# A selective-scan stack with two multiplications per job on another engine, table blocks with a settled queue ahead of them, and zeros around the closing of a sum

## The chip, the cores and the metric

The kernel runs on one core of a Trainium2 chip. A core has a matmul engine (PE, with its weight loads shown as PEld), a vector engine (DVE), a scalar engine (ACT), a general engine (POOL) and a queue that issues transfers (SP). They run side by side and wait for each other by semaphores; each works through its own instructions in program order. Matmul results lie in PSUM, which POOL does not read here; everything else lies in SBUF or in device memory. The metric is the device time of one execution in microseconds (us): lower is better.

## The reference, cut to what matters

A batch of 8 images of 192 x 56 x 56 goes through four layers, each a residual of a group norm and a block. Layer 0 is an involution. Layers 1 to 3 are selective scans over the 3136 pixels of an image, and take nearly all of the time:

```python
xc = silu(conv4(xz[:d]) + conv_b)                    # four taps along the sequence
dt, B, C = split(xc @ x_proj)                        # rank, 16, 16
delta = softplus(dt @ dt_proj + dt_b)
h = exp(delta * A) * h + delta * xc * B              # step by step along the sequence, 16 states per channel
y = (h * C).sum(over states) + xc * D
out = (y * silu(z)) @ out_proj
```

In layer 1 the 192 channels are three slices of 64 that share their weights (512 inner channels each), with layer norms over the 192 before and after and a projection behind; layers 2 and 3 have 384 inner channels.

## The kernel before

An image is cut into 7 chunks of 448 pixels. A **job** is one chunk of one sequence: in layer 1 there are three jobs per chunk (kinds 0, 1 and 2, one per slice), 168 in all; in layers 2 and 3 one per chunk, 56 each. Inner channels go in groups of 128 (`nd` = 4 in layer 1, 3 in layers 2 and 3), and each group in four **units** (`q` = 0 to 3): 128 partitions hold 32 channels by 4 states, four such sets (`NR`) side by side. A job has 16 units (12 in layers 2 and 3), and all layers together 4032. `m` is the number of a unit within its job.

For unit k, `ssm_layer`'s loop issues these (the line numbers are those of the profile):

- `decays` (L712, ACT): `da` = exp(delta x A), four instructions, into two PSUM tiles, one for each half of the unit; there is no second pair of tiles, so each half waits for the scan that used it before.
- `spread_b` (L706, PE): the row of B, spread over the partitions, into one PSUM tile `b`.
- `inputs_lo` (L729, DVE): the first half of the scan's inputs `uhg` = (delta x) times B, with B from `b`. `inputs_hi` (L725, POOL): the second half, with B from `rows`, which a transfer brought to SBUF.
- `scan` (L733, DVE): two per unit, one for each half.
- `keep` (L737, ACT) saves the last state; `inputs_begin` (L720, ACT) puts it in front of a later unit.
- `readout` (L742, POOL): the scanned states times C, two per unit.
- `reduce` (L748 for the D term at q = 0, L751, PE): adds the states up into one PSUM tile `y` per group. At q = 3 the sum is closed. `gated` (L767, DVE) then multiplies it with the gates; it stands in the loop in units with q = 3, when the `reduce` of the unit before has closed a sum.

The work is staggered: loop k issues scan k, the inputs of k + 1 on DVE and of k + 2 on POOL, the readout of k - 2, and the reduction of k - 3. So the loop with q = 2 closes a sum.

Between these, the loop issues the **steps** that prepare the next job and finish the one before: in two places per unit, `plan[2 * m]` ahead of the first scan and `plan[2 * m + 1]` ahead of the second. A `Step` has matmuls, a rest that evicts them, a cost, and `left`: before the step runs, the rests still open are run until no more than `left` of them remain. `places` spreads a list of steps over a stretch of places by their costs. A step that is a `block` goes only into a first place of a unit. The steps that prepare a job (`project_steps`): convs (L576 evicts them), the silu block, `xproj`, the splitting of B into parts (`left_of_b`, L595), the deltas (L618; L623 evicts), the softplus block (L626), then `x_again` and `dtx` (L630, L633), whose results are stored (`store`) and loaded again as the `rep` operands of the next job's units (`load_ops`, L697). Both blocks change ACT's table and change it back (`table_block`, L579, L552, L626); the silu block also does the gates of the running job (L560). With them go the job-specific steps: in layer 1 a layer norm ahead of kind 0 and, for a finished chunk, a layer norm and a projection (L530, L538, L976, L982), which stand in the running job of kind 0; in layers 2 and 3 the input projection. Two PSUM tiles (`mm`) hold all results of steps in turn.

`nothing` (L757) adds matmuls with zero weights into an open sum `y`; the loop calls it at up to three points of a unit whose steps have little matmul work (`more`), never in a loop that closes a sum.

Of the kernel before, what the change touches and what calls it, by code (L numbers as in the profile page):

```python
# [21 lines left out]
T = RC * WW  # L22
# [17 lines left out]
class Step:  # L40


    def __init__(self, matmuls, rest, left, cost=None, block=False):
        self.matmuls, self.rest, self.left, self.block = matmuls, rest, left, block
        self.cost = cost if cost is not None else 1.0 if matmuls else 0.3
        self.closes = block


def pause(cost=1.0):
    return Step(None, lambda: None, 9, cost)  # L50


class Steps:
# [20 lines left out]
def conv_mamba_stack(ctx: ExitStack, tc: tile.TileContext, a, out):  # L74
    nc = tc.nc
# [488 lines left out]
    def project_steps(pool, w, u, conv_mm, conv_cost, running=None, meanwhile=()):  # L564


        nd, rank = w.nd, w.rank
        nk = rank + 2 * NS

        def conv(j):  # L570
            if j == 0:
                u.xc = pool.tile([128, nd, T], F32, tag="xc", name="xc", bufs=2)
            u.cps[j] = conv_mm(j)

        def conv_out(j):
            nc.scalar.activation(u.xc[:, j, :], u.cps[j][:, :T], AF.Identity, bias=w.convb[:, j : j + 1])  # L576

        def silu():
            with_gates(lambda: nc.scalar.activation(u.xc, u.xc, AF.Silu), running)  # L579
# [12 lines left out]
        def left_of_b(m):  # L592
            u.left[m] = mm_tile()
            rows = NS if m == 0 else 96
            nc.tensor.matmul(u.left[m][:NS, :T], lhsT=ident[:NS, :NS], rhs=u.dbl[:NS, :], start=True, stop=False)  # L595
            nc.tensor.matmul(u.left[m][:NS, :T], lhsT=minus[:rows, m, :], rhs=u.parts[:rows, :], start=False, stop=True)

        def part_of_b(m):
            p0 = 32 * m + 32
            nc.scalar.copy(u.parts[p0 : p0 + NS, :], u.left[m][:NS, :T])  # L600

        def rows_out():

# [12 lines left out]
        def delta(j):  # L616
            u.dps[j] = mm_tile()
            nc.tensor.matmul(u.dps[j][:, :T], lhsT=w.dtw[:, j * 128 : (j + 1) * 128], rhs=u.dbl[:nk, :], start=True, stop=True)  # L618

        def delta_out(j):  # L620
            if j == 0:
                u.dt = pool.tile([128, nd, 2, T], F32, tag="dt", name="dt")
            nc.scalar.activation(u.dt[:, j, 0, :], u.dps[j][:, :T], AF.Identity, bias=w.dtb[:, j : j + 1])  # L623

        def softplus():
            table_block(lambda: nc.scalar.activation(u.dt[:, :, 0, :], u.dt[:, :, 0, :], AF.Softplus))  # L626

        def x_again(j):
            u.xps[j] = mm_tile()
            nc.tensor.matmul(u.xps[j][:, :T], lhsT=ident, rhs=u.xc[:, j, :], start=True, stop=True)  # L630

        def dtx(j):
            nc.vector.tensor_mul(u.dt[:, j, 1, :], u.dt[:, j, 0, :], u.xps[j][:, :T])  # L633

        def store(j):
            u.ops[j] = dram.tile([128, 2, T], F32, tag="ops", name="ops", bufs=8)
            nc.sync.dma_start(out=u.ops[j], in_=u.dt[:, j])

        u.ops, u.cps, u.dps, u.xps, u.left = {}, {}, {}, {}, {}
        deltas = [Step(lambda j=j: delta(j), lambda j=j: delta_out(j), 1) for j in range(nd)]  # L640

        stores = [Step(lambda j=j: x_again(j), lambda j=j: dtx(j), 1 if j > 1 else 9) for j in range(nd)]
        stores[1].closes = True
        return (
            [Step(lambda j=j: conv(j), lambda j=j: conv_out(j), 1, conv_cost) for j in range(nd)]
            + [pause(), Step(None, silu, 0, 0.3, block=True), *meanwhile, Step(xproj, xproj_out, 1, nd), pause(0.5)]
            + [Step(lambda: left_of_b(0), lambda: part_of_b(0), 0, 1.3)] + deltas[:1] + [Step(None, rows_out, 2)] + deltas[1:2]
            + [Step(lambda: left_of_b(1), lambda: part_of_b(1), 1, 1.3)] + deltas[2:]
            + [pause(0.3), Step(None, softplus, 0, 0.3, block=True)],
            stores[:2] + [Step(None, lambda: store(0), 1)] + stores[2:3] + [Step(None, lambda: store(1), 1)]  # L650
            + stores[3:] + [Step(None, lambda j=j: store(j), nd - 1 - j) for j in range(2, nd)]
        )
# [22 lines left out]
    def ssm_layer(pool, w, jobs, n_slots):  # L675
# [23 lines left out]
                    )  # L699
                reps[g].append(t)  # L700

        def spread_b(k):

            i, j, q = units[k]
            brow[k] = banks.b.tile([128, 512], F32, tag="b", name="b")
            nc.tensor.matmul(brow[k][:, :T], lhsT=pick_b[:, q, :], rhs=us[i].parts, start=True, stop=True)  # L706

        def decays(k, h):
            i, j, q = units[k]
# [6 lines left out]
        def inputs_begin(k):  # L716
# [2 lines left out]
            before = zeros[:, :NR] if jobs[i][1] else carry[jobs[i][0]][:, j, q, :]  # L719
            nc.scalar.copy(uhg[k][:, :, 0:1], before.unsqueeze(2))  # L720

        def inputs_hi(k):
            i, j, q = units[k]
            b = us[i].rows[0, q].unsqueeze(1).to_broadcast([128, 2, T])
            nc.gpsimd.tensor_mul(uhg[k][:, 2:4, 1:], reps[k // NQ][1][:, :, 1, :], b)  # L725

        def inputs_lo(k):
            b = brow[k][:, :T].unsqueeze(1).to_broadcast([128, 2, T])
            nc.vector.tensor_mul(uhg[k][:, 0:2, 1:], reps[k // NQ][0][:, :, 1, :], b)  # L729

        def scan(k, h):
            v = uhg[k][:, 2 * h : 2 * h + 2, :].rearrange("p r t -> p (r t)")
# [19 lines left out]

        def nothing(k, n):

            if k >= 0 and units[k][2] < NQ - 1:
                for _ in range(n):
                    nc.tensor.matmul(  # L757
                        ys[k // NQ][:, : nd * 112], lhsT=zeros, rhs=w.dd.rearrange("p j e -> p (j e)")[:, : nd * 112],
                        start=False, stop=False,
                    )  # L760

        def load_of(steps):
            return sum(st.cost for st in steps if st.matmuls)
# [3 lines left out]
            nc.vector.tensor_mul(us[i].zs[:, j, :], us[i].zs[:, j, :], ys[g][:, :T])  # L767

        n_places = 2 * per_job

        ready = n_places - (13 if nd == 4 else 9)

        def places(*stretches):


            plan = [[] for _ in range(n_places)]
            for steps, first, end in stretches:
                todo, debt = list(steps), 0.0
# [11 lines left out]
        bg = Steps()  # L790
        for i, u in enumerate(us):
            u.parts = parts[i % 2]
        steps, stores = jobs[0][2](us[0])
        bg.run(steps + stores + jobs[0][3](us[0]))
        bg.flush()
        for q in range(NQ):
            us[0].row_in(0, q)
# [20 lines left out]
        for k, (i, j, q) in enumerate(units):  # L818
            m = k % per_job
            if m == 0:  # L820

                fetch, outs, rest = tail
                if i + 1 < len(jobs):
                    u = us[i + 1]
                    steps, stores = jobs[i + 1][2](u, us[i], outs)
                    plan = places((steps, 0, ready), (stores, ready, ready + 3), (rest + jobs[i + 1][3](u), ready + 3, n_places))
# [110 lines left out]
    def mamba_jobs(pool, w):  # L937
# [3 lines left out]
        for ck in cks:  # L941
# [48 lines left out]
            for i in range(3):  # L990

                def prepare(u, *beside, i=i, ck=ck, norm=norm):
# [6 lines left out]
                            )  # L999
                        return pm  # L1000

                    steps, stores = project_steps(pool, w, u, conv_mm, 2, *beside)
                    return (norm() + steps, stores + [Step(None, lambda: chunks.fetch_next(ck), 2)]) if i == 0 else (steps, stores)

                def gates(u, i=i, ck=ck):
                    def z_mm(j):
# [29 lines left out]
    def dense_jobs(pool, w, layer):  # L1036
# [3 lines left out]
        for ck in cks:  # L1040
# [11 lines left out]
            def prepare(u, *beside, c=c, ck=ck, in_mm=in_mm):  # L1052
# [17 lines left out]
                def conv_mm(j):  # L1070
# [5 lines left out]
                steps, stores = project_steps(pool, w, u, conv_mm, 4, *beside)  # L1076
                return (
                    [Step(None, gnorm, 2)]
                    + [pause(), Step(None, lambda: chunks.fetch_next(ck), 2)]
                    + [Step(lambda j=j: xin(j), lambda j=j: xin_out(j), 1 if j else 0, 2) for j in range(w.nd)]  # L1080
                    + steps, stores,
                )

            def gates(u, in_mm=in_mm):
# [110 lines left out]
```

## Time and profile before

| | |
|---|---|
| median of three runs | 27277.67 us (27261.01 to 27288.59) |
| profiled execution, its own time | 27303.25 us |
| its span, first to last instruction | 27301.5 us |
| mean granted clock of PE | 0.825 of full |
| L742 on POOL: 8064 of 1929 ns | 15382.5 us |
| L712 on ACT: 16128 of 636 ns | 10262.8 us |
| L751 on PE: 32256 | 4977.9 us |
| L757 on PE (zeros): 5002, in pairs | 2777.4 us |

A group's row gives line, engine, operation, result and operands with their shapes, the count, the busy time and the mean of one, and then the idle time of the engine just ahead of these instructions, with what ended most of it. A row of waits gives who waited for whom, the time in all, how often, and the longest. A row of the timeline gives the start, the time it took, and in brackets the idle time before it. In a row of stretches come, behind the stretch, its length, the busy time (and count) of PE, PEld, DVE, ACT and POOL, the granted clock, the share of the transfer engines and GB/s.

### The profile page before, as it was taken

How to read it: one execution, taken by the hardware profiler on the slowest of the kernel's cores; microseconds unless marked ns; L12 is line 12 of the kernel's file. 1: busy time of each engine (PE TensorE's matmuls, PEld its weight loads, DVE VectorE, ACT ScalarE, POOL GpSimd, SP SyncE). 2: the span in 40 equal slices, each digit the busy share in tenths (PEclk: the TensorE clock that was granted, in tenths of full speed). 3: DMA queues.
4: the chain of work that ended last, by engine and by line, in shares of the span. 5: the costliest groups of instructions: out<-in, count | busy, mean ns of one | idle time of the engine just before them, and what ended most of it. 6: DMA issues, size and time to landing. Idle time of an engine off the chain costs nothing. (4 is left out here: it accounts for less than half of the span.)

```text
span 27301.5 us, 247072 instructions
## 1 busy us (share of the span) xinstructions
PE 22204.6 (81%) x73722; PEld 6925.3 (25%) x73722; DVE 22794.6 (83%) x17677; ACT 17015.0 (62%) x32354; POOL 24237.5 (89%) x12820
## 2 busy tenths in 40 slices
PE   9987777777777787777877877788888887888888
PEld 3322222222222222222222222222222222222222
DVE  8878888888888888888888888887888887888888
ACT  1146666666666666666666666665666666666666
POOL 4478999999999989999999999987999998999999
PEclk9987787777777778777778787778888888888888
DMA  4433333333333333333333333333333333333343
GB/s 106 108 104 113 117 117 115 115 115 120 116 115 114 118 113 116 116 117 114 118 113 117 117 115 113 120 112 108 128 125 128 129 130 117 130 131 132 133 133 121
DMA packets 1249487, 3236.36 MB, mean 119 GB/s; under 512 B 170924, under 2 KB 510916, under 8 KB 1248008
## 3 DMA queue, kind: packets, MB, share of 16 engines
q1 hardware_dynamic: 1245336, 3219.49, 36.0%
q8 instruction: 579, 9.49, 0.1%
q14 instruction: 772, 6.32, 0.1%
q10 hardware_dynamic: 2800, 1.06, 0.0%
HBM read 2502.68 MB, written 555.55 MB: 112 GB/s over the span
## 5 line engine op out<-in xcount | busy, mean ns | idle before, releaser
L733 DVE TENSOR_TENSOR_SCAN uhg<-da,uhg 128x898 f32<-128x898 f32 x8064 | 16075.9, 2013 | 1624.0 <-ACT da L712 1622.0
L742 POOL TENSOR_TENSOR uhg<-uhg,rows 128x896 f32<-128x896 f32 x8064 | 15382.5, 1929 | 1390.3 <-ACT carry L737 1093.2
L712 ACT ACTIVATE da<-rep,k 128x448 f32<-128x448 f32 x16128 | 10262.8, 636 | 1901.4 <-DVE uhg L733 1584.4
L725 POOL TENSOR_TENSOR uhg<-rep,rows 128x896 f32<-128x896 f32 x4032 | 8403.9, 2084 | 794.9 <-DMA rep<-ops 710.8
L751 PE MATMUL y<-uhg,k 128*32 128x448 f32 x32256 | 4977.9, 665 | 177.7 <-POOL uhg L742 175.8
L729 DVE TENSOR_TENSOR uhg<-rep,b 128x896 f32<-128x896 f32 x4032 | 4287.9, 1063 | 498.5 <-PE b L706 449.6
L737 ACT COPY carry<-uhg 128x4 f32<-128x4 f32 x4032 | 790.9, 196 | 5110.6 <-DVE uhg L733 5107.9
L706 PE MATMUL b<-k,k 96*128 96x448 bf16 x4032 | 1598.7, 396 | 2178.5 <-DVE uhg L729 2178.3
L757 PE MATMUL y<-w_d,k 128*128 128x448 f32 (+1 forms) x5002 | 2777.4, 652 | 0.0
L748 PE MATMUL y<-xc,w_d 128*128 128x448 f32 x2016 | 1362.3, 767 | 1112.5 <-DVE zs L767 1112.3
L996 PE MATMUL mm<-xs,k 128*128 128x448 f32 x2688 | 1292.5, 606 | 661.3 <-ACT da L712 380.4
L633 DVE TENSOR_TENSOR dt<-dt,mm 128x448 f32<-128x448 f32 x1008 | 602.5, 617 | 1273.7 <-ACT dt L626 1007.7
L1046 PE MATMUL mm<-v,w_in 96*128 96x448 f32 x2688 | 1467.6, 678 | 243.5 <-ACT zs L659 135.6
L751 PEld LDWEIGHTS y<-uhg,k 128*32 128x32 f32 x32256 | 728.4, 117 | 3501.8 <-issue 1574.1
L757 PEld LDWEIGHTS y<-w_d,k 128*128 128x128 f32 x5002 | 1038.0, 226 | 1783.4 <-issue 1771.7
L423 POOL TENSOR_TENSOR x<-x,one 96x448 f32<-96x448 f32 x560 | 633.0, 1134 | 651.7 <-DVE one L415 634.1
L618 PE MATMUL mm<-dbl,w_dt 36*128 36x448 f32 (+1 forms) x2016 | 1204.4, 706 | 0.3 <-ACT dt L623 0.3
L630 PE MATMUL mm<-xc,k 128*128 128x448 f32 x2016 | 1123.7, 675 | 85.3 <-DVE dt L633 84.8
L706 PEld LDWEIGHTS <-k 96*128 96x128 bf16 x4032 | 418.8, 104 | 2677.4 <-issue 1622.5
L415 DVE TENSOR_TENSOR prod<-mm,shifted 128x448 f32<-128x448 f32 x1680 | 933.3, 611 | 190.5 <-PE mm L403 170.1
L1073 PE MATMUL mm<-xin,w_conv 128*128 128x448 f32 x2688 | 1087.6, 547 | 0.3 <-ACT xin L657 0.2
L623 ACT ACTIVATE dt<-mm,k 128x448 f32<-128x448 f32 x1008 | 616.7, 626 | 710.9 <-PE mm L618 710.3
(134 smaller groups left out, 20276.8 us busy)
## 6 DMA issues: line engine op xcount, KB each, us to landing
rep<-ops SPq DMA_DIRECT2D x4032, 448.0 KB, 4.8
rows<-bc SPq DMA_DIRECT2D x2240, 224.0 KB, 5.2
ops<-dt SPq DMA_DIRECT2D x1008, 448.0 KB, 2.6
shifted<-xpad SPq DMA_DIRECT2D x672, 179.0 KB, 4.6
xg<-stream SPq DMA_DIRECT2D x168, 336.0 KB, 3.4
xr<-stream SPq DMA_DIRECT2D x168, 336.0 KB, 4.8
stream<-xr SPq DMA_DIRECT2D x112, 336.0 KB, 3.2
xs<-xg SPq DMA_DIRECT2D x224, 112.0 KB, 2.3
```

The costliest lines, as they stand in the source:

```text
L618: nc.tensor.matmul(u.dps[j][:, :T], lhsT=w.dtw[:, j * 128 : (j + 1) * 128], rhs=u.dbl[:nk, :], start=True, stop=True)
L706: nc.tensor.matmul(brow[k][:, :T], lhsT=pick_b[:, q, :], rhs=us[i].parts, start=True, stop=True)
L712: nc.scalar.activation(t[:, 64 + 449 * r : 512 + 449 * r], reps[k // NQ][h][:, r, 0, :], AF.Exp, scale=w.neg_a[:, j * NR + 2 * h + r, q : ...
L725: nc.gpsimd.tensor_mul(uhg[k][:, 2:4, 1:], reps[k // NQ][1][:, :, 1, :], b)
L729: nc.vector.tensor_mul(uhg[k][:, 0:2, 1:], reps[k // NQ][0][:, :, 1, :], b)
L733: nc.vector.tensor_tensor_scan(v, banks.da[h][:, 63:961], v, 0.0, ALU.mult, ALU.add)
L742: nc.gpsimd.tensor_mul(v, v, us[i].rows[1, q].unsqueeze(1).to_broadcast([128, 2, T]))
L748: nc.tensor.matmul(ys[k // NQ][:, :T], lhsT=w.dd[:, j, :], rhs=us[i].xc[:, j, :], start=True, stop=False)
L751: nc.tensor.matmul(y[32 * r : 32 * r + 32, :T], lhsT=fold, rhs=uhg[k][:, r, 1:], start=False, stop=(q == NQ - 1))
L757: nc.tensor.matmul(ys[k // NQ][:, : nd * 112], lhsT=zeros, rhs=w.dd.rearrange("p j e -> p (j e)")[:, : nd * 112], start=False, stop=False,)
L996: nc.tensor.matmul(pm[:, :T], lhsT=w.inconv[:, k, j * 128 : (j + 1) * 128], rhs=ck.xs[:, i, 2 - 2 * k : 2 - 2 * k + T], start=(k == 0), st ...
L1046: nc.tensor.matmul(pm[:, :T], lhsT=w.inw[:, k, m * 128 : (m + 1) * 128], rhs=ck.v[:, k, :], start=(k == 0), stop=(k == NCT - 1),)
```

## The change

1. `by_vector` names units: in layer 1 m = 1 and 15 of a job, in layers 2 and 3 m = 11, not the very first two units. There `inputs_hi` does nothing, and `inputs_lo` multiplies both halves on DVE with `b`.
2. `settle` is a new step of cost 2 that does nothing, has `left` = 0, and goes only into the second place of a unit. One stands at the end of the convs and one at the end of the deltas, in place of pauses. The list of steps is cut into more pieces, and `bounds` gives each piece its own stretch of places: the silu block begins at place 8 (layers 2 and 3), 10 (for a job of kind 0) or 6, and the softplus block at 6 or 8 places later; it was only bounded by `ready` before.
3. A loop that closes a sum calls `nothing` ahead of `reduce`, up to two, into the sum that is about to be closed; and `spread_b` in such a loop leaves `b` open and adds a matmul with zeros behind it, if the unit's steps have little matmul work.

```diff
+def settle(cost=2.0):
+    step = Step(None, lambda: None, 0, cost)
+    step.settles = True
+    return step
...
             [Step(lambda j=j: conv(j), lambda j=j: conv_out(j), 1, conv_cost) for j in range(nd)]
-            + [pause(), Step(None, silu, 0, 0.3, block=True), *meanwhile, Step(xproj, xproj_out, 1, nd), pause(0.5)]
+            + [settle()], [Step(None, silu, 0, 0.3, block=True), *meanwhile] + [Step(xproj, xproj_out, 1, nd)] * (nd == 3),
+            [Step(xproj, xproj_out, 0, nd)] * (nd == 4) + [pause(1.0 if nd == 4 else 3.5)]
...
-            + [pause(0.3), Step(None, softplus, 0, 0.3, block=True)],
+            + [settle()], [Step(None, softplus, 0, 0.3, block=True)],
...
-        def spread_b(k):
+        def spread_b(k, nothing=False):
...
-            nc.tensor.matmul(brow[k][:, :T], lhsT=pick_b[:, q, :], rhs=us[i].parts, start=True, stop=True)
+            nc.tensor.matmul(brow[k][:, :T], lhsT=pick_b[:, q, :], rhs=us[i].parts, start=True, stop=not nothing)
+            if nothing:
+                nc.tensor.matmul(
+                    brow[k][:, : nd * 112], lhsT=zeros, rhs=w.dd.rearrange("p j e -> p (j e)")[:, : nd * 112], start=False, stop=True
+                )
...
+        def by_vector(k):
+            return k > 1 and k % per_job in ((1, 15) if nd == 4 else (11,))
...
         def inputs_hi(k):
+            if by_vector(k):
+                return
...
-            nc.vector.tensor_mul(uhg[k][:, 0:2, 1:], reps[k // NQ][0][:, :, 1, :], b)
+            for h in range(2 if by_vector(k) else 1):
+                nc.vector.tensor_mul(uhg[k][:, 2 * h : 2 * h + 2, 1:], reps[k // NQ][h][:, :, 1, :], b)
...
-        ready = n_places - (13 if nd == 4 else 9)
+        def bounds(job):
+            silu = 8 if nd == 3 else 10 if job[0] == 0 else 6
+            softplus = silu + (6 if nd == 3 else 8)
+            return 0, silu, silu + 2, softplus, softplus + 1, softplus + 4, n_places
...
-                        if todo[0].block and p % 2 and p < end - 1:
+                        if (todo[0].block if p % 2 else todo[0].settles) and p < end - 1:
...
+            more = 3 - math.ceil(load_of(plan[2 * m] + plan[2 * m + 1]))
+            closing = q == 2
+            if closing:
+                nothing(k - 4, min(more, 2))
             if k >= 3:
                 reduce(k - 3)
-
-            more = 3 - math.ceil(load_of(plan[2 * m] + plan[2 * m + 1]))
...
-                spread_b(k + 2)
+                spread_b(k + 2, closing and more > 0)
```

The rest of the diff hands the longer list of pieces through (`prepare` of `mamba_jobs` and `dense_jobs`, `places`).

More of the change, by code (lines that the diff above doesn't have):

```diff
@@ L46, in __init__ @@
         self.closes = block
+        self.settles = False
 def pause(cost=1.0):
     return Step(None, lambda: None, 9, cost)
+def settle(cost=2.0):
+    step = Step(None, lambda: None, 0, cost)
+    step.settles = True
+    return step
 class Steps:
@@ L792, in ssm_layer @@
             u.parts = parts[i % 2]
-        steps, stores = jobs[0][2](us[0])
-        bg.run(steps + stores + jobs[0][3](us[0]))
+        bg.run(sum(jobs[0][2](us[0]), []) + jobs[0][3](us[0]))
         bg.flush()
@@ L824, in ssm_layer @@
                     u = us[i + 1]
-                    steps, stores = jobs[i + 1][2](u, us[i], outs)
-                    plan = places((steps, 0, ready), (stores, ready, ready + 3), (rest + jobs[i + 1][3](u), ready + 3, n_places))
+                    at = bounds(jobs[i + 1])
+                    plan = places(*zip((*jobs[i + 1][2](u, us[i], outs), rest + jobs[i + 1][3](u)), at, at[1:]))
                 else:
@@ L1000, in conv_mm @@
                         return pm
-                    steps, stores = project_steps(pool, w, u, conv_mm, 2, *beside)
-                    return (norm() + steps, stores + [Step(None, lambda: chunks.fetch_next(ck), 2)]) if i == 0 else (steps, stores)
+                    convs, *others, stores = project_steps(pool, w, u, conv_mm, 2, *beside)
+                    if i == 0:
+                        return norm() + convs, *others, stores + [Step(None, lambda: chunks.fetch_next(ck), 2)]
+                    return convs, *others, stores
                 def gates(u, i=i, ck=ck):
@@ L1074, in conv_mm @@
                     return pm
-                steps, stores = project_steps(pool, w, u, conv_mm, 4, *beside)
+                convs, *others = project_steps(pool, w, u, conv_mm, 4, *beside)
                 return (
@@ L1080, in prepare @@
                     + [Step(lambda j=j: xin(j), lambda j=j: xin_out(j), 1 if j else 0, 2) for j in range(w.nd)]
-                    + steps, stores,
+                    + convs, *others,
                 )
```

## The prediction

> **What bounds the kernel now.** I read the page's parts 1 and 5, then the waits of DVE, then the timeline around the longest waits.
>
> ```profile
> PE 22204.6 (81%) x73722; PEld 6925.3 (25%) x73722; DVE 22794.6 (83%) x17677; ACT 17015.0 (62%) x32354; POOL 24237.5 (89%) x12820
> ...
> L733 DVE TENSOR_TENSOR_SCAN uhg<-da,uhg 128x898 f32<-128x898 f32 x8064 | 16075.9, 2013 | 1624.0 <-ACT da L712 1622.0
> ...
> L725 POOL TENSOR_TENSOR uhg<-rep,rows 128x896 f32<-128x896 f32 x4032 | 8403.9, 2084 | 794.9 <-DMA rep<-ops 710.8
> ...
> L729 DVE TENSOR_TENSOR uhg<-rep,b 128x896 f32<-128x896 f32 x4032 | 4287.9, 1063 | 498.5 <-PE b L706 449.6
> ```
>
> POOL is the busiest engine, but it is not at its limit. A unit (one `k`) keeps POOL 5.82 us: one multiply L725, and two L742 of which a pair takes 3.82 us. DVE needs 4.84 us: two scans and one L729. Over a chunk of layer 1 (48 units, three jobs) the scan starts in the trace give 303.1 us, of which POOL is busy 279.5 and DVE 254.7. So POOL's 23.6 us of idle time and DVE's 48.4 come together: DVE stands still at a few places per job, POOL runs out of scanned units, and both then run on. The bound is the chain DVE-ACT, broken by these stops, with POOL close behind. The stops:
>
> ```profile
> DVE uhg L733 <- ACT da L712: 1622.0, 616, 4.9
> DVE dt L633 <- ACT dt L626: 1007.7, 255, 40.3
> DVE uhg L729 <- PE b L706: 449.6, 421, 2.6
> DVE dt L633 <- PE mm L630: 258.7, 145, 5.4
> DVE xr L982 <- PE mm L976: 219.6, 57, 5.7
> DVE y L530 <- PE mm L524: 207.1, 56, 8.7
> ```
>
> The first two rows are the silu and softplus blocks, one each per job. ACT loads a table, works, loads the old table again, and only then makes the decays `da` for the next scan. One silu block of layer 1:
>
> ```profile
> 6014.40 1.30 ACT L712 ACTIVATE da<-rep,k 128x448 f32<-128x448 f32 x2
> 6015.64 1.14 ACT L576 ACTIVATE xc<-mm,k 128x448 f32<-128x448 f32 x2
> 6016.80 1.28 ACT L579 ACT_TABLE_LOAD   x1
> 6018.09 1.70 ACT L579 ACTIVATE xc<-xc 128x1792 f32<-128x1792 f32 x1
> 6019.70 1.68 ACT L560 ACTIVATE zs<-zs 128x1792 f32<-128x1792 f32 x1
> 6021.39 1.28 ACT L552 ACT_TABLE_LOAD   x1
> 6022.69 1.31 ACT L712 ACTIVATE da<-rep,k 128x448 f32<-128x448 f32 x2
> ...
> 6024.03 2.03 DVE L733 TENSOR_TENSOR_SCAN uhg<-da,uhg 128x898 f32<-128x898 f32 x1 [4.40 <-ACT da L712]
> ```
>
> The two conv evictions (L576, 1.14 us) stand between the last decays and the table load, so all of their time is in DVE's 4.40 us.
>
> **The change, part by part.** I worked out by the planner's rules in which half unit every step falls, before and after. m is the unit in the running job; in layer 1 the jobs go round three kinds, 0, 1, 2.
>
> *Silu block.* `settle` has the last convs evicted in the second half of the unit before. There ACT has room: per unit its decays take 2.6 us, its two small copies 0.4, of 4.84. The 1.14 us leave the stop: 4.40 becomes 3.3 in kinds 0 and 1, 4.93 becomes 3.8 in kind 2. 1.1 x 168 jobs = **-185 us**. In layers 2 and 3 (4.0 us now, two evictions in front) I take -1.0 x 112 = **-112**.
>
> *Softplus block.* Before, the last delta matmuls and their evictions stand in the block's own place, and `dtx` waits behind it. Layer 3:
>
> ```profile
> 25239.85 0.63 ACT L623 ACTIVATE dt<-mm,k 128x448 f32<-128x448 f32 x1 [1.69 <-PE mm L618]
> ...
> 25243.15 0.62 DVE L633 TENSOR_TENSOR dt<-dt,mm 128x448 f32<-128x448 f32 x1 [2.76 <-ACT dt L626]
> ...
> 25245.77 2.03 DVE L733 TENSOR_TENSOR_SCAN uhg<-da,uhg 128x898 f32<-128x898 f32 x1 [2.00 <-ACT da L712]
> ```
>
> ACT waits for PE, evicts, and then only loads. Mean stops from the trace's times: kind 0 4.0 us (1.15 of it the last `dtx`, behind PE), kind 1 4.8, kind 2 6.2, layer 2 6.3, layer 3 7.0. After, ACT begins the table load about 1.6 us (carry copy, decays) behind the scan before. Loads and softplus take 4.3 us in layer 1, 3.9 in 2 and 3; the next decays 1.3. So `da` is there 7.2 (6.8) us behind that scan; DVE's own work until then is 4.9, 0.6 for the gates in a unit with q = 3, and one or two `dtx` of 0.6. What is left is 0.5 to 1.1 us. That is the low end. At the high end the deltas, now packed into fewer places with two mm buffers, run at half clock (L618: a pair is 1.02 us fast, 1.86 slow), the evictions hold ACT up by 2 us, and little is won. I take 2.5, 2.5 (the last `dtx` stays), 1.7, and 2.5 in layers 2 and 3, nearer to the low end because the clock is 0.8 to 1.0 in the units before. -(1.5 + 2.3 + 4.5) x 56 chunks = **-465**; -4.0 x 112 = **-450**.
>
> *Layer norm at the end of a chunk (kind 0).* Its steps move two units earlier, and DVE's part comes a whole unit behind PE's. The centring (L530, 3.64 us of waiting now) finds its average done: -3.6. The second `add` (L982) comes half a unit later than now. Here PE's clock decides:
>
> ```profile
> 7797.23 0.68 DVE L982 SCALAR_TENSOR_TENSOR xr<-mm,k,xr 96x448 f32<-96x448 f32 x1 [4.19 <-PE mm L976]
> ...
> 7765.00:7800.00 35.00, 31.09 (x64) 7.65 (x64) 24.79 (x20) 15.37 (x30) 25.62 (x14) 0.50 0.26 86
> ```
>
> PE is busy for 31.09 of these 35 us and the granted clock (third from the right) is 0.50 throughout. The new plan has zeros in only one unit between the average and the projections, so I let the projections stay slow (4.79 us for six): PE ends the second 7.5 us into its unit, DVE asks for it about 2 us earlier; 3.64 becomes 2.2. Together -5.0 x 56 = **-280**. The wait for the scale (2.53) stays. The Trainium skill, "TensorE: Matmul & The Clock Gate", Part 1, has the clock doubled after some 3.4 us of sustained matmuls. The row contradicts it for these matmuls of 64 rows. By the rule the second add would not wait at all, some 120 us less in all; I go by the row.
>
> *Multiplications moved.* By the indices, 168 x 2 - 1 = 335 in layer 1 and 112 in layers 2 and 3. DVE pays its start-to-start of L729, 0.98 us each: **+328** and **+110**, nothing hides it. POOL gives up 447 x 2.08 = 931 us. It has idle time in every job, so this wins nothing by itself; it is what lets POOL keep up with jobs of 97 instead of 101 us (89 us of work instead of 93). In layers 2 and 3 POOL's next job begins with a wait:
>
> ```profile
> 25255.63 2.07 POOL L725 TENSOR_TENSOR uhg<-rep,rows 128x896 f32<-128x896 f32 x1 [5.80 <-DMA rep<-ops]
> ```
>
> It is 11.9 us behind `dtx` 0 (25243.77) by store and reload, and the moved multiply is just ahead of it, so its 2 us turn into waiting. POOL then trails until the silu stop; PE's reductions queue behind POOL, and `b` and the gates behind them. The nearest waits are 0.25 to 0.5 us in m 2 and 3 now. Bounds 0 and 4 us per job; I take **+2.0** x 112 = **+224**, also for the three convs now packed into m 1 and 2 (8 passes, 3 us each, beside 1.3 us of PE's own work per unit of 4.85).
>
> *Zeros.* About 2000 more, 24 per chunk in layer 1 and 6 per job in 2 and 3. Each is two passes, 0.75 us fast, 1.5 slow, and alone they cost nothing while PE waits (it waits 0.7 to 3.3 us in most of these units). In front of a closing up to two delay the sum that the gates (DVE) need one unit later: PE has 0.85 us to spare behind the new pair of convs in m 1 when fast, and is 3 us late when slow. Below nothing, they keep PE fast. For this, the conv pairs and xproj a unit earlier, in layer 1: bounds -1 and +9 per chunk, taken **+1.5** x 56 = **+84**.
>
> *Sum.* Layer 1: -185 - 465 - 280 + 328 + 84 = -518. Layers 2 and 3: -112 - 450 + 110 + 224 = -228. Together -746: 27303 (the profiled execution; its span 27301.5) becomes 26557. The median of the runs is 26 us below that execution: **26,530 us**.
>
> **Rivals.**
> *Cheap ends.* Softplus at its minimum (a further -2 per chunk and -1.5 per job), no trailing, no new waits: -112, -168, -224, -84, 25,940 at best; half of it 26,240. For: the clock is 0.9 to 1.0 in m 0 to 3. Against: POOL's work, 67.8 us per job in layers 2 and 3, leaves little below 72.
> *Half is given back.* PE is slow before the softplus in kinds 0 and 1, which then win nothing (3.8 x 56 = +213), and in the conv pairs (another 3 us per chunk, +168): 26,910. For: the clock of 0.5 in m 7 of these kinds. Against: the zeros now in m 6.
> *Slower.* One mechanism: PE falls to half clock in m 0 to 2 and m 4 to 6 of layer 1, where convs and deltas are now packed. Then ACT's evictions hold back the decays, softplus wins nothing in layer 1 (+465), the closing behind two zeros makes the gates wait 3 us in two jobs a chunk (+336), and half of layers 2 and 3's gain goes (+200): 27,530. It decides from a mean clock below about 0.65 there (0.84 to 1.0 now; 0.5 in m 7 and m 11 to 15 shows how easily it goes).
> *It doesn't do what it says.* The stops only move: DVE's idle time, 4507 us in all, must fall by 438 to pay for the multiplications. If it falls by just that: 27,280.
>
> **How the numbers follow.** Forecast 0.50, cheap ends 0.12, half given back 0.14, no change 0.06, slower 0.18. 0.2% (55 us) is about what a measurement of this kernel can tell from no change. Faster 0.76, same 0.06, slower 0.18. The range leaves out the slower case and the very cheapest: 26,120 to 27,260. The forecast's own is 26,300 to 26,800.
>
> **What will show it.** Right: the DVE waits L733 for L712 and L633 for L626 fall to about 1200 and 250 us, L530 is gone, L742 has the same count, L725 447 fewer; DVE's busy share passes 87% and equals POOL's within a few points. Wrong: L729 waiting for L706, or L767 for L751, above 700 us; L633 for L626 still near 1000; a clock below 0.80 in layer 1.

## The result, and the profile after

The changed kernel takes 26856.92 us (median of four runs, 26820.56 to 26869.98), against 27269.34 of the kernel before on the same chip: a ratio of 0.9849 [0.9832, 0.9866]. The change gains 412 us, where the forecast's sum had 746. The profiled execution took 26820.56 us, its span 26818.8.

The page of the changed kernel, part 1 and the same three groups of part 5. Line numbers have moved: the scan is L753, POOL's multiply L744, DVE's L749, the decays L725.

```profile
PE 22711.2 (85%) x77664; PEld 7503.5 (28%) x77664; DVE 23259.5 (87%) x18124; ACT 17035.2 (64%) x32354; POOL 23358.0 (87%) x12373
...
L753 DVE TENSOR_TENSOR_SCAN uhg<-da,uhg 128x898 f32<-128x898 f32 x8064 | 16061.4, 2013 | 917.2 <-ACT da L725 908.5
...
L744 POOL TENSOR_TENSOR uhg<-rep,rows 128x896 f32<-128x896 f32 x3585 | 7485.6, 2088 | 853.8 <-DMA rep<-ops 820.8
...
L749 DVE TENSOR_TENSOR uhg<-rep,b 128x896 f32<-128x896 f32 x4479 | 4738.1, 1066 | 827.2 <-PE b L715 585.9
```

POOL has 447 multiplies fewer and DVE 447 more. Both engines now stand at 87 %, so neither is a hard limit. The scans wait for the decays 908.5 us instead of 1622.0. But the multiply on DVE waits for `b` longer than before, and the waits of DVE show where that comes from:

```profile
DVE uhg L753 <- ACT da L725: 908.5, 672, 3.9
DVE uhg L749 <- PE b L715: 585.9, 476, 3.8
DVE xr L1128 <- PE mm L1122: 340.9, 112, 3.6
...
DVE zs L788 <- PE y L771: 280.2, 120, 7.9
DVE dt L641 <- PE mm L638: 255.0, 225, 2.4
DVE uhg L749 <- PE b L717: 183.8, 78, 2.7
DVE dt L641 <- ACT dt L634: 156.2, 57, 40.3
```

The two rows for ACT (L753, L641) have fallen as a table block that waits less should make them fall. In their place stand rows that name PE: `b` by its own matmul (L715) and by the zeros put behind it (L717), and the gates (L788) by the sum `y`. PE is busy 85 % and yet late. One softplus block of kind 0 shows why, here as the timeline of PE, with two of DVE's waits, in m 5 to 7:

```profile
7670.96 0.92 PE L603 MATMUL mm<-dbl,k 16*16 16x448 f32 x2 [2.51 <-ACT dbl L596]
...
7673.80 1.86 PE L626 MATMUL mm<-dbl,w_dt 36*128 36x448 f32 x2
...
7675.59 1.67 PE L603 MATMUL mm<-dbl,k 16*16 16x448 f32 x2
...
7677.66 1.86 PE L778 MATMUL y<-w_d,k 128*128 128x448 f32 x2
...
7679.46 1.72 PE L771 MATMUL y<-uhg,k 128*32 128x448 f32 x8
...
7681.11 3.35 PE L626 MATMUL mm<-dbl,w_dt 36*128 36x448 f32 x4
7681.25 0.62 DVE L788 TENSOR_TENSOR zs<-zs,y 128x448 f32<-128x448 f32 x1 [2.57 <-PE y L771]
...
7684.74 1.70 PE L717 MATMUL b<-w_d,k 128*128 128x448 f32 x2
...
7686.48 1.09 DVE L749 TENSOR_TENSOR uhg<-rep,b 128x896 f32<-128x896 f32 x1 [2.67 <-PE b L717]
```

and the same three units as stretches, with the granted clock third from the right:

```profile
7668.90:7673.80 4.90, 2.84 (x6) 0.59 (x6) 4.90 (x5) 4.43 (x10) 4.90 (x3) 0.87 0.04 12
7673.80:7681.80 8.00, 8.00 (x17) 1.92 (x17) 5.43 (x6) 4.05 (x9) 7.97 (x5) 0.50 0.11 30
7681.80:7692.80 11.00, 11.00 (x32) 3.52 (x30) 6.17 (x6) 8.81 (x13) 6.32 (x4) 0.65 0.41 146
```

In m 6 PE is busy for all of 8.00 us at a clock of 0.50, so a pair of matmuls takes nearly twice its time (1.86 us, against 1.02 at the full clock). The new zeros (1.86 us, L778) stand ahead of the closing sum that the gates wait for, and the zeros on B's row (1.70 us, L717) ahead of the multiply. Means over the middle chunks of layer 1, from the scan starts: a chunk takes 298.2 us instead of 303.1.

### The profile page after: what moved, and what is told of

Its sections match the earlier page's. It is cut to its first block, busy times and chain, and to the rows that moved or that the text cites. A ratio compares the mean times of both kernels' runs of the same rounds, so it can differ in the third digit from the quotient of the medians.

```text
span 26818.8 us, 255069 instructions
## 1 busy us (share of the span) xinstructions
PE 22711.2 (85%) x77664; PEld 7503.5 (28%) x77664; DVE 23259.5 (87%) x18124; ACT 17035.2 (64%) x32354; POOL 23358.0 (87%) x12373
## 4 chain that ended last, share of the span: by engine, by line
PE 32%; DVE 32%; ACT 15%; issue 13%; DMA 4%; POOL 3%; SPq 1%; DVEq 0%; POOLq 0%; ACTq 0%
DVE uhg L753 21%; DVE uhg L749 8%; ACT da L725 6%; PE mm L626 5%; PE y L771 4%; PE mm L1102 3%; PE mm L411 3%; PE mm L603 2%; PE y L778 2%; POOL uhg L762 2%; PE mm L1075 2%; DMA rows<-bc 2%; DMA rep<-ops 2%; PE y_inv L446 2%; ACT L560 2%
## 5 line engine op out<-in xcount | busy, mean ns | idle before, releaser
L753 DVE TENSOR_TENSOR_SCAN uhg<-da,uhg 128x898 f32<-128x898 f32 x8064 | 16061.4, 2013 | 917.2 <-ACT da L725 908.5
L725 ACT ACTIVATE da<-rep,k 128x448 f32<-128x448 f32 x16128 | 10260.9, 636 | 1850.8 <-DVE uhg L753 1536.6
L744 POOL TENSOR_TENSOR uhg<-rep,rows 128x896 f32<-128x896 f32 x3585 | 7485.6, 2088 | 853.8 <-DMA rep<-ops 820.8
L749 DVE TENSOR_TENSOR uhg<-rep,b 128x896 f32<-128x896 f32 x4479 | 4738.1, 1066 | 827.2 <-PE b L715 585.9
L771 PE MATMUL y<-uhg,k 128*32 128x448 f32 x32256 | 4570.2, 627 | 46.2 <-POOL uhg L762 44.5
L778 PE MATMUL y<-w_d,k 128*128 128x448 f32 (+1 forms) x7718 | 3898.9, 611 | 0.0
L715 PE MATMUL b<-k,k 96*128 96x448 bf16 x4032 | 1576.6, 391 | 1696.8 <-DVE uhg L749 1688.7
L778 PEld LDWEIGHTS y<-w_d,k 128*128 128x128 f32 x7718 | 1571.9, 221 | 2176.8 <-issue 2147.6
L768 PE MATMUL y<-xc,w_d 128*128 128x448 f32 x2016 | 1273.6, 721 | 543.9 <-DVE zs L788 542.5
L1075 PE MATMUL mm<-v,w_in 96*128 96x448 f32 x2688 | 1406.5, 654 | 232.2 <-ACT zs L668 128.6
L626 PE MATMUL mm<-dbl,w_dt 36*128 36x448 f32 (+1 forms) x2016 | 1471.2, 839 | 48.6 <-ACT k L608 48.2
L715 PEld LDWEIGHTS <-k 96*128 96x128 bf16 x4032 | 405.1, 100 | 2842.3 <-issue 1406.7
L641 DVE TENSOR_TENSOR dt<-dt,mm 128x448 f32<-128x448 f32 x1008 | 605.2, 618 | 600.8 <-PE mm L638 255.0
L603 PE MATMUL mm<-dbl,k 16*16 16x448 f32 x1120 | 700.0, 713 | 340.5 <-ACT dbl L596 340.5
```

The lines of the kernel that those rows point to most:

```text
L725: nc.scalar.activation(t[:, 64 + 449 * r : 512 + 449 * r], reps[k // NQ][h][:, r, 0, :], AF.Exp, scale=w.neg_a[:, j * NR + 2 * h + r, q : ...
L749: nc.vector.tensor_mul(uhg[k][:, 2 * h : 2 * h + 2, 1:], reps[k // NQ][h][:, :, 1, :], b)
L753: nc.vector.tensor_tensor_scan(v, banks.da[h][:, 63:961], v, 0.0, ALU.mult, ALU.add)
L771: nc.tensor.matmul(y[32 * r : 32 * r + 32, :T], lhsT=fold, rhs=uhg[k][:, r, 1:], start=False, stop=(q == NQ - 1))
L778: nc.tensor.matmul(ys[k // NQ][:, : nd * 112], lhsT=zeros, rhs=w.dd.rearrange("p j e -> p (j e)")[:, : nd * 112], start=False, stop=False,)
L1075: nc.tensor.matmul(pm[:, :T], lhsT=w.inw[:, k, m * 128 : (m + 1) * 128], rhs=ck.v[:, k, :], start=(k == 0), stop=(k == NCT - 1),)
```

## The experiments

Each kernel was run beside the kernel before. A ratio, and a gain over the kernel before, is to the median of that kernel's runs on the same chip (27265.87 to 27292.36 us); that these medians lie 26 us apart says how little a small difference between kernels of two chips means.

**Without the zeros at closings.**

```diff
-                nothing(k - 4, min(more, 2))
+                pass
-                spread_b(k + 2, closing and more > 0)
+                spread_b(k + 2)
```

> The change without its zeros in units that close a sum (none ahead of the closing, none behind the row of B); all else as in the change. Theory: in the unit ahead of the softplus block (m 6 of kinds 0 and 1 in layer 1) PE runs at half clock, and a zero takes 1.86 us ahead of the closing and 1.70 us behind B, both in front of something DVE waits for (2.57 and 2.67 us in the trace of the change). Without them about 3.5 us go in two jobs of each of 56 chunks, some 400 us: 26,450 to 26,650, with the waits of the gates for y near 50 us. Rival: the zeros hold PE's clock up elsewhere and are worth more than that: slower than the change, 27,000 or more, clock in layer 1 back at 0.80 from 0.84.

Measured: 26631.51 us, 0.9762 [0.9747, 0.9778]. The zeros cost 225 us in the change (26856.92 - 26631.51). The gates' row is what they did most visibly; in this kernel it is

```profile
DVE zs L788 <- PE y L771: 35.5, 31, 7.0
```

instead of 280.2. The zeros do hold PE's clock up (0.860 over the whole program with them, 0.835 without), and the time is worse for it: a higher mean clock is not the aim.

**Without the moved multiplications.**

```diff
-            return k > 1 and k % per_job in ((1, 15) if nd == 4 else (11,))
+            return False
```

> The change without the moved multiplications: all second halves of the inputs stay on POOL. Theory of the prediction: the chain DVE-ACT is the bound, so DVE gets 447 x 0.98 us back and POOL has room: 26,420 to 26,600, POOL's share about 91%. Rival: POOL close behind is the bound of stretches, and its relief pays for the multiplications: no faster than the change, 26,850 to 27,150, with more waiting of PE's reductions for POOL and of DVE for b and y.

Measured: 26638.3 us, 0.9763 [0.9743, 0.9782], 38 us above the range. They cost 219 us here.

**The new places and `settle` alone** (both edits above).

> The kernel before with the new places and the settle steps alone: no moved multiplications, no zeros in closing units. Theory: both left-out parts cost time, so this is the fastest of the four, 26,050 to 26,350. Rival: the new places bring DVE ahead of POOL, which then holds it: 26,700 to 27,000.

Measured: 26473.13 us, 0.9702 [0.9685, 0.9719], between the two theories. So the places gain 815 us; on top of them the multiplications cost 158 (first kernel less this one), the zeros 165 (second less this one), and both together 384 (the change less this one), 60 more than the two apart.

**The moved multiplications alone**, in the kernel before.

> The kernel before with the moved multiplications alone. Theory: DVE pays 438 us, POOL's relief is worth nothing where DVE stands still anyway: 27,550 to 27,700. Rival: POOL is the bound of the kernel before: 26,900 to 27,150.

Measured: 27799.17 us, 1.0191 [1.0174, 1.0208], dearer than either theory: +511 us for 447 multiplies whose own cost on DVE is 438.

**The change without zeros in the closing of m 6 in layer 1**, to see whether the one place shown above is all of their cost.

```diff
-            closing = q == 2
+            closing = q == 2 and not (nd == 4 and m == 6)
```

> The change without the zeros of one closing unit alone: m 6 in layer 1, the unit ahead of the softplus block. Theory: the whole loss from the zeros is there, because PE is at half clock in that unit; elsewhere they are free or useful (kind 2 lost 1.3 us per job when all were taken out). So no slower than the version without any of them: 26,560 to 26,650. Rival: the zeros cost a little in every closing unit: 26,720 to 26,800.

Measured: 26761.85 us, 0.981 [0.9794, 0.9825]. That is 95 us of the 225; the gates' wait falls to 80.4 us. The other 130 us lie elsewhere. By DVE's idle time most of them stand in m 0 of kind 1: 2.79 us per job in this kernel, 0.90 without any of the zeros.

**More zeros a unit earlier**, in m 5 of kinds 0 and 1, first in the change, then on the places alone: if only a want of work let the clock fall, this should lift it.

```diff
-            nothing(k - 3, more > 2)
+            nothing(k - 3, 3 if nd == 4 and m == 5 and i % 3 < 2 else more > 2)
```

> The change, with three more zeros per job of kinds 0 and 1 (layer 1, m 5), into the open sum, where PE waits 2.5 us for the eviction of xproj and then falls to half clock. Theory: the half clock of m 6 and 7 is what spoils the softplus block; with PE busy through the gap the clock in m 6 goes from 0.50 to over 0.85, the waits for y and b there vanish, and 4 to 8 us per such job go: 26,000 to 26,450. Rival: the order of evictions and matmuls over two mm buffers holds ACT up whatever the clock: 26,800 to 26,950.

> The new places alone (no moved multiplications, no zeros in closing units), with the same three zeros in m 5 of kinds 0 and 1. Theory of the clock: 4 us per such job of the 26,473 of the places alone go, 26,000 to 26,250. Rival (order of evictions): 26,430 to 26,520.

Measured: 26670.75 us, 0.9773 [0.9756, 0.979], and 26294.08 us, 0.9638 [0.9623, 0.9652]. They gain 186 and 179 us. In the change the clock of m 6 rises from 0.50 to 0.65 (kind 0) and from 0.54 to 0.75 (kind 1); on the places alone from 0.58 to 0.93 in kind 0, and only from 0.51 to 0.57 in kind 1. Less than expected both times: more matmuls a unit earlier help, but PE falls back in kind 1.

**`xproj` of layers 2 and 3 a place later**, because the out-projection's add (L1128, 340.9 us of waiting in the change) was a stop that I had not foreseen.

```diff
-            + [settle()], [Step(None, silu, 0, 0.3, block=True), *meanwhile] + [Step(xproj, xproj_out, 1, nd)] * (nd == 3),
-            [Step(xproj, xproj_out, 0, nd)] * (nd == 4) + [pause(1.0 if nd == 4 else 3.5)]
+            + [settle()], [Step(None, silu, 0, 0.3, block=True), *meanwhile],
+            [Step(xproj, xproj_out, 0, nd), pause(1.0 if nd == 4 else 0.5)]
```

> The new places alone, with xproj of layers 2 and 3 moved from the second place of m 4 to the first place of m 5, so that DVE's add of the output projection (3.0 us of waiting for PE per job, L1128) comes after the scans of m 4. Theory: that wait lies under the silu stop, whose decays come 3.2 us after DVE is free anyway, so it moves to the wait of the scan for ACT and the time stays within 60 us of 26,473. Rival: the wait is paid in full and goes: about 26,150.

Measured: 26455.37 us, 0.9698 [0.9681, 0.9714]; 18 us beside the places alone, no difference that can be told. But the wait is not gone. On the places alone, and in this kernel, its row is

```profile
DVE xr L1128 <- PE mm L1122: 363.9, 112, 3.6
DVE xr L1128 <- PE mm L1122: 331.5, 220, 1.8
```

Now two adds per job wait, behind one more scan, because the matmuls of the output projection themselves end late. So the run does not show what the wait costs. That most of it lies under the silu stop is read from the trace of the places alone: in one job of layer 2 a scan follows the add, the next one starts at 20416.82 us, and the decays for that one come from behind the silu block only at 20416.18. So without the wait some 0.6 us of that job could go, not 3.

**The same matmuls with more rows.** The stretch at half clock holds matmuls that use few rows, that is, operands that fill few of the 128 partitions: 16 (L603) and 36 (L626). On the places alone, the first matmul of `left_of_b` and the deltas get operands of 128 rows, filled up with zeros; for this `xproj` gets 128 columns. The number of matmuls, their 448 columns of data and the results stay.

```diff
-        w.xproj = pool.tile([128, nd, w.rank + 2 * NS], F32, tag="w_x", name="w_x")
+        w.xproj = pool.tile([128, nd, 128], F32, tag="w_x", name="w_x")
+        nc.vector.memset(w.xproj, 0.0)
...
-        w.dtw = pool.tile([2 * NS + w.rank, nd * 128], F32, tag="w_dt", name="w_dt")
+        w.dtw = pool.tile([128, nd * 128], F32, tag="w_dt", name="w_dt")
...
-        nk = rank + 2 * NS
+        nk = 128
...
-            u.dbl = pool.tile([44, T], F32, tag="dbl", name="dbl", bufs=2)
+            u.dbl = pool.tile([128, T], F32, tag="dbl", name="dbl", bufs=2)
...
-            nc.tensor.matmul(u.left[m][:NS, :T], lhsT=ident[:NS, :NS], rhs=u.dbl[:NS, :], start=True, stop=False)
+            nc.tensor.matmul(u.left[m][:NS, :T], lhsT=ident[:, :NS], rhs=u.dbl, start=True, stop=False)
```

> The new places alone, with the matmuls of xproj, of the splitting of B and of the deltas widened by zero rows and columns to 128 (the same streams of 448 columns, the same results): before, they use 16 or 36 of 128 rows. It asks what makes PE's clock fall ahead of the softplus block. Theory of rows: matmuls with few rows don't keep the clock up although PE is busy, so with full rows the clock in m 6 of kinds 0 and 1 goes from 0.55 to over 0.85 and the time to 26,150 to 26,350. Rival, theory of the gap: it is PE's wait of 2.5 us in m 5 alone, which stays; clock 0.5 to 0.6, time 26,430 to 26,520.

Measured: 25545.51 us, **0.9359 [0.934, 0.9378]**, the best of all the kernels, and far more than either theory gave. A stretch of kind 1 (m 5, 6, 7), in the kernel with the places alone:

```profile
7664.30:7669.10 4.80, 2.80 (x4) 0.75 (x5) 4.80 (x4) 4.05 (x9) 4.80 (x3) 0.64 0.05 12
7669.10:7676.60 7.50, 7.50 (x17) 1.61 (x16) 5.55 (x6) 4.42 (x9) 7.50 (x5) 0.50 0.00 0
7676.60:7686.90 10.30, 10.30 (x32) 3.24 (x31) 6.38 (x7) 8.12 (x12) 6.39 (x4) 0.71 0.60 202
```

The same units with the wider operands:

```profile
7399.20:7404.00 4.80, 2.80 (x5) 0.84 (x6) 4.80 (x5) 4.06 (x9) 4.80 (x3) 0.76 0.05 12
7404.00:7409.30 5.30, 5.30 (x20) 1.93 (x18) 5.30 (x5) 4.48 (x10) 5.30 (x4) 0.89 0.00 0
7409.30:7417.20 7.90, 7.55 (x31) 2.44 (x29) 6.16 (x7) 7.77 (x12) 7.90 (x5) 1.00 0.82 288
```

In m 5 PE is busy for the same 2.80 us in both, and waits 2.50 and 2.54 us for ACT ahead of `left_of_b`. The clock there is 0.64 and 0.76; some of the widened matmuls stand in this unit already. In the next unit it is busy all the time in both. With few rows the clock stays at 0.50 and the unit takes 7.50 us; with 128 it goes to 0.89 and the unit takes 5.30. In these two jobs the clock falls in or just behind PE's wait both times; what differs is how long it stays down. The stretches at half clock, first with few rows, then with 128:

```profile
7665.60:7682.66 17.06, 16.36 (x34) 3.88 (x34) 13.49 (x10) 11.23 (x23) 14.09 (x8) 0.50 0.18 59
7401.70:7405.11 3.41, 3.41 (x7) 1.34 (x6) 3.41 (x3) 2.07 (x5) 3.41 (x3) 0.50 0.07 17
```

Over the middle 52 chunks the clock falls in m 5 or 6 of all 104 jobs of kinds 0 and 1 with few rows, and stays down for 10.24 to 17.07 us; with 128 rows it falls in 44 of them, all of kind 1, for 3.41 us. The deltas of layer 1 as a group of the kernel with the places alone (count, then busy time and mean ns):

```profile
L626 PE MATMUL mm<-dbl,w_dt 36*128 36x448 f32 x1344 | 1037.2, 894 | 0.0
```

and the deltas of all layers with the wider operands:

```profile
L627 PE MATMUL mm<-dbl,w_dt 128*128 128x448 f32 x2016 | 1020.1, 602 | 58.6 <-ACT k L609 54.3
```

The matmul with over three times the rows is faster, 602 ns against 894 (those of layers 2 and 3, of 44 rows, had taken 876 with the places alone). By the scan starts a chunk goes from 293.0 to 280.5 us and the jobs of layers 2 and 3 from 73.93 and 72.62 to 72.71 and 70.30: 56 x (12.5 + 3.5) = 900 us, of the 928 measured.

Few rows do not always bring the clock down, though. Layer 0 has matmuls of 32 rows, which in the kernel before (L403) take 106.7 and 39.2 us between 1000 and 1200 us, more than all other matmuls there together, and the clock is full:

```profile
1000.00:1200.00 200.00, 198.61 (x1088) 72.71 (x1086) 176.10 (x334) 25.84 (x48) 98.33 (x87) 1.00 0.47 106
```

PE hardly waits there, and the mix is another one. Which of these makes the difference was not tested, so what is shown is that the wider operands bring the clock up in this place, not a rule for rows.

**The same, with yet more zeros** in m 5 of kinds 0 and 1 and at the end of kind 0's m 15.

```diff
-            nothing(k - 3, more > 2)
+            nothing(k - 3, 3 if nd == 4 and m == 5 and i % 3 < 2 else more > 2)
...
-            nothing(k - 3, more > 1)
+            nothing(k - 3, 3 if nd == 4 and m == 15 and i % 3 == 0 else more > 1)
```

> As e9, and also the three zeros in m 5 of kinds 0 and 1, and two more zeros at the end of m 15 of kind 0, behind the gates, so that the convs of the next job start at full clock (1.2 us of waiting for b in m 0 of kind 1). If rows count: 25,950 to 26,150, the lowest of all. If only the gap counts: 26,200 to 26,290, little below the 26,294 of the zeros in m 5 alone.

Measured: 25760.87 us, 0.9437 [0.9414, 0.9459], 215 us slower than without them. In m 0 of kind 1, just behind the added zeros, the clock is 0.50 (0.90 without), and the multiplies in m 0 and 1 wait 1.81 and 3.56 us for `b`. The zeros do not make it fall: in both kernels it has fallen in m 14 and is at 0.50 through m 15. Without the zeros it is mostly back as m 0 begins, with them only in m 1; why later, with more matmuls, stays open. So the version with the places and the wider operands, and nothing else of the change, is the fastest that was found.

**The whole change with the wider operands.** If POOL bounds the wide version, taking 447 multiplies from it should now gain.

> The whole change (moved multiplications and zeros in closing units included) with the matmuls of xproj, B's splitting and the deltas at 128 rows, as in e9. In e9 POOL stands still for only 0.4 us per job of kinds 0 and 2 in layer 1. Theory, POOL has become the bound there: the moved multiplications now pay, 25,200 to 25,450. Rival, the chain DVE-ACT is still the bound (its stops are 26 us per chunk, none of them for POOL): they cost up to 438 us more than the 25,546 of e9, 25,700 to 26,000.

Measured: 26309.53 us, 0.9646 [0.9629, 0.9664]: 764 us slower than the places with the wider operands, beyond both theories. The run brings back the zeros as well, and the two were not separated here; together they do not pay. That is no proof that POOL was not the bound: in layer 1, taken as one stretch of the kernel with the places and the wider operands, POOL is busy for 15506.21 of 15600 us:

```profile
1800.00:17400.00 15600.00, 12283.03 (x41768) 3885.24 (x41766) 14109.48 (x9828) 10894.09 (x20787) 15506.21 (x8012) 0.85 0.37 125
```

So a shorter chunk would need less work on POOL: 48 units of the prediction's 5.82 us are 279.4 of the 280.5 us. But what POOL gives up, DVE does not make good. POOL's wait for a scanned unit, in the kernel with the places and the wider operands:

```profile
POOL uhg L763 <- ACT carry L758: 75.7, 109, 5.6
```

and in the whole change with the wider operands:

```profile
POOL uhg L763 <- ACT carry L758: 1359.7, 977, 5.0
```

With 447 more multiplies and the zeros DVE falls behind, and POOL waits for it. Per chunk of layer 1 the period grows by 11.5 us: 5.9 are the multiplies themselves (the prediction's 328 us over 56 chunks), 5.0 are added stops of DVE, above all for `b` in m 0 of kind 1 (0.39 to 1.86 us) and for the gates in m 6 (0.63 and 0.86 us where there were none). The clock in m 6 is 0.79 and 0.78 instead of 1.00 and 0.91, though there are more zeros; why is open.

**The kernel before with the wider operands alone.**

> The kernel before with the same widened matmuls alone: none of the change. If PE's clock ahead of the softplus block was a large part of that stop already before (mean stops of 4 to 7 us per job), about 2 to 3 us per job go: 26,500 to 26,800. If the stop of before is its place in the plan (deltas and evictions inside the block), little goes without the new places: 27,050 to 27,250.

Measured: 26702.57 us, 0.9787 [0.9765, 0.9809]. Wider operands alone gain 563 us, the places alone 815, both together 1729: 351 more than the sum. So the two depend on each other. The clock in m 9 of kinds 0 and 1, where the last deltas stand, goes from 0.80 and 0.76 to 1.00; in m 7, behind a wait of PE, it stays at half with the wider operands too (0.52 and 0.57, from 0.51). That the new places pack the deltas more densely, and so need a fast PE more, is the likely reason; it was not tested by itself.

## Why the prediction was right in direction and half wrong in size

Stops are mean idle time of DVE per job, from the traces.

- **Silu block: exact.** 3.3, 3.3 and 3.8 us were expected in kinds 0, 1, 2; 3.32, 3.30 and 3.85 came. In layers 2 and 3, where 3.0 was expected, DVE stands still for 3.1 and 3.4 us at this place, but by then mostly for the out-projection's add (L1128), which I had not foreseen. One of those of layer 1 in the changed kernel:

```profile
7664.06 2.03 DVE L753 TENSOR_TENSOR_SCAN uhg<-da,uhg 128x898 f32<-128x898 f32 x1 [3.33 <-ACT da L725]
```

- **Softplus block in layer 1: the step that failed.** I took 2.5, 2.5 and 1.7 us "because the clock is 0.8 to 1.0 in the units before". Kind 0 came to 7.78 (3.98 before), kind 1 to 5.83 (4.79), kind 2 to 3.08 (6.19). That is 10.0 us per chunk more than expected, 56 x 10.0 = 560 us, more than the whole miss of 327 us (26856.92 against 26,530); other steps gave some of it back. The waits behind the new zeros in m 6 and 7 are part of it: without the zeros (the first experiment) the stops are 4.57, 4.57 and 4.37 us, still 6.8 us per chunk or some 380 us over. The clock I read belonged to what PE did there *before*; the change brings the deltas and the parts of B into those units, and with these matmuls the clock is 0.50 and 0.54. The high end that I had written down was the case. My rival "half is given back" (26,910) had named this mechanism for these two kinds, and the measured 26,857 is nearer to it than to the forecast, in part by luck: it also had the pairs of convs at half clock, and the clock in m 0 to 2 of these kinds is 0.89 to 1.00. The wider operands turn that around (0.50 to 0.89 in the stretch above, m 6 from 7.50 to 5.30 us). With the places alone the three stops are 4.80, 5.44 and 4.68 us, with the wider operands 2.55, 2.33 and 1.29, about what I had expected of them. So on the new places the operands' width decides the clock, and the clock the stop. The edit also widened `xproj`'s columns, and which of the three widened matmuls counts most was not separated.
- **Softplus in layers 2 and 3: in part.** 2.5 us expected, about 3.9 came (6.2 and 7.0 before), 0.45 of it the multiply's wait for `b`. PE's clock is 0.62 to 0.68 there. With the places and the wider operands it is 1.00, and the stop 2.0.
- **Layer norm: more than expected.** -5.0 us expected, -7.3 came: the second `add` hardly waits any more. I let the projections stay slow; they ran fast, three pairs in 2.49 us, where the average (64 rows, 64 columns) is still slow:

```profile
7710.18 4.74 PE L532 MATMUL mm<-sq,k 64*64 64x448 f32 x6 [2.27 <-ACT sq L540]
...
7722.81 2.49 PE L1003 MATMUL mm<-y,w_proj 64*96 64x448 f32 x6
```

The stretch that I had shown from before, PE busy 31.09 of 35.00 us at 0.50, is not met again: in 35 us from 7705.00 on PE is busy 25.16 us at 0.70. So matmuls of 64 rows do not always run at half clock. The Trainium skill, "TensorE: Matmul & The Clock Gate", Part 1 ("What's actually happening"), has the clock set by how busy PE has been, and doubled after some 3.4 us of sustained matmuls. What I had worked out from it for the second add (no wait) came true. For the softplus unit, PE busy 8.00 of 8.00 us at 0.50, it does not hold as it stands.
- **Moved multiplications.** +438 was DVE's own time. Measured: +511 alone, +219 in the change, +158 on the places. So the 931 us less on POOL did buy something on the new places, but less than they cost, in both versions with these places; in the kernel before it bought nothing. (By the sum a job of layer 1 would have come to 98 us, not to the 97 that I wrote; nothing rests on it.)
- **Trailing in layers 2 and 3.** +2.0 us per job; the multiply's wait for `b` in m 2 alone is 1.63 and 1.40. The size came out by luck: with the places alone, where no multiplication is moved, that wait is 1.56 and 1.74. So the moved multiply, which my working had start it, is not its cause; the packed convs, which the term named besides, are left as the likely one. Against the kernel without them the moved multiplications cost 0.78 and 0.51 us per job, some 72 us in both layers, where 110 + 224 had been set down. The two layers together gained 215 us (228 expected), by errors that cancel: the softplus blocks gave about 300 us instead of 450.
- **Zeros.** +84 expected, +225 in the change and +165 on the places. I had priced both clocks and chosen near the fast one; in m 6 of kinds 0 and 1 the slow one was granted: the same fault as with the softplus.
- **What would show it.** L744 447 fewer, L530's wait gone, the decays' wait 908.5 (about 1200 expected), L641 for ACT 156.2 (about 250; another 123.8 us of its waiting stand in a row that names the decays L725), DVE and POOL both 87 %: as said. `b` came to 585.9 + 183.8 = 770 us, over the 700 that I had named as wrong; that sign pointed at the right fault. The other sign for it, a clock below 0.80 in layer 1, did not: it is 0.84 (0.79 before), because a mean over the layer hides single units.

By the scan starts layer 1 gained 274 us (518 expected) and layers 2 and 3 215 (228): nearly all of the miss is in layer 1. (These are of the profiled executions, which lie 483 us apart, the medians 412.) The rival that the stops only move is refuted by DVE's idle time, which fell from 4507 to 3559 us (span less busy time).

## What to carry to other kernels

Before work is packed into fewer places, read the PE clock of the stretch where *that kind of work* runs now, not that of the stretch it goes to. A step that is moved off a stop is worth what the next engine lets it be worth: here the same plan gained 815 us or, with PE quick enough to follow it, 1157 (25545.51 against 26702.57). Zeros that keep PE warm are paid for wherever they stand ahead of something that another engine waits for; in this kernel filling up the rows of matmuls that were there anyway did more, at no cost that these runs show.

## What was not expected of the hardware

- PE can be busy all the time and be granted half clock: 8.00 of 8.00 us at 0.50 in the change, 7.50 of 7.50 on the places alone, with matmuls of 16 and 36 rows mixed with others of 128. With 128 rows, most of them zeros, the unit of the places alone ran at 0.89, and a delta took 602 ns instead of 894. Few rows are not enough for it: in layer 0, with matmuls of 32 rows, the clock is 1.00. The wider operands gained 2.1 % in the kernel before and 3.5 % on the new places (25545.51 against 26473.13); no cost of them shows in these runs.
- More matmuls did not always mean more clock: with the zeros added in the version with yet more of them, a unit just behind them was at 0.50 that was at 0.90 without them. No run explains this.
